# Another order of GpSimd's sums, ScalarE's ReLUs, VectorE's block sums and second-layer products around a seven-product pointwise convolution

## The chip, the core and the metric

The kernel runs on one NeuronCore of a Trainium2 chip. TensorE multiplies matrices into PSUM; VectorE and ScalarE read and write both PSUM and SBUF; GpSimd works on SBUF alone; SyncE issues most of the transfers. Each engine takes its own instructions in the order in which the program has them, and engines wait for each other at semaphores. The metric is the time of one execution on the device in microseconds (us).

## What is computed

Four images of 256 channels and 64x64 points (4096 points each), all in float32. The reference, cut to what matters here:

```python
# layer 0: attention over 4096 points
attn = softmax(q @ k)                       # q, k: 32 channels
x = gamma * (v @ attn.T) + x
# layer 1: clustering, then an MLP and a pointwise convolution
y = x + ls1 * cluster(group_norm(x, gn1_w, gn1_b))
hdn = conv1x1(group_norm(y, gn2_w, gn2_b), mlp_w1, mlp_b1)     # 256 -> 1024
hdn = conv1x1(gelu(hdn), mlp_w2, mlp_b2)                       # 1024 -> 256
y = y + ls2 * hdn
z = relu(batch_norm(y * dw_w))
z = relu(batch_norm(conv1x1(z, pw_w)))                         # 256 -> 256
```

The change lies in the last five lines, the MLP with what follows it.

## The kernel before

The images are worked on one after the other; for each there is an attention stage, a clustering stage and an MLP stage (`mlp`, from line 1144). The order of all instructions is written out by hand: the program runs under a manual schedule, so that each engine's queue is the order in which the Python code issues its instructions.

The MLP stage goes over blocks of 512 points, `nb` = 0 to 7 (image 2 has only blocks 0 to 6 here; its block 7 is done by `late_block` beside the next image's attention). Within a block, `j` = 0 to 3 goes over pairs of 128 hidden channels, `j` and `j + 4`. Each product of two 256-channel operands is done as a 2x2 scheme of seven half-size products in place of eight: the operand's quarters are 128 channels by 256 points (`quarters`), and sums of quarters are formed ahead (`factors`, L1230 to L1233) and block sums behind.

- `first(nb, j, ...)` does the seven first-layer products through `seven` (L1351 is the matmul, `product`). They go into three PSUM buffers called `hp`, `hq` and `hr` with 2, 3 and 2 products, which are taken in turn from a pool of two (`ps_s`). ScalarE copies one product out (L1359), VectorE makes the seven block sums (`plus`, L1342), ScalarE applies gelu to the four quarters of `hs` (L1306), in the order h4, h2, h1, h3.
- The second layer's products lag by one `j`: `second_by_seven` is a generator with seven products (L1266), and GpSimd's four sums of the quarters of `hs` (L1273, L1274, L1279, L1280) between them. `seven` draws from it at four places (`mo`): before `hp`, between `hp` and `hq`, between `hq` and `hr`, and after `hr`. How many products are drawn at each is the tuple `slots`: (0, 2, 2, 3) usually, (3, 1, 2, 1) after a score and at `j` = 2 with a pointwise convolution.
- `finish(nb - 1)` puts the second layer's parts of the block before together, on VectorE during the next block's `j` = 0 and 1: three sums (L1409 to L1411), two scaled sums (L1396, 128x256), and two more (L1396, 128x512), which wait in a list `drips` and are issued one at a time behind a `plus`. The ReLUs of both channel halves (`relu`, L1387, ScalarE) wait in a list `hooks`, which `hook()` empties at the end of `j` = 1.
- `norm(nb + 1)` scales the next block's input on VectorE (L1176, two instructions) and leaves its four sums to GpSimd (`ahead`), issued at `j` = 2's generator. `own` are the four sums for the pointwise convolution of the block before; before the change they are issued one by one in `j` = 1's generator.
- `pointwise(nb - 1)`, at `j` = 2 of the middle blocks, does the pointwise convolution by seven products (buffers `hp_pw`, `hq_pw`, `hr_pw`), with its block sums on VectorE (L1342 too), its ReLUs on ScalarE (L1218) and its outputs sent from SyncE's queue (`leave`).
- In images 0 to 2 the next image's first scores are made in the same stage: after `j` = 3 two PSUM buffers from the same pool of two are filled by `score` (L363), ScalarE copies them to SBUF (L371, L372), and VectorE takes maxima of 512 columns (L376), which wait in a list `maxima` and are issued by `rest()`, one at a call.

Two places say the order of L376 and of the ReLUs:

```python
                if j == 3:
                    rest()
...
                hs = first(nb, j, todo, slots, pw)
                if j != 1:
                    rest()
...
                elif j == 1:
                    assert not drips
                    hook()
```

Of the kernel before, what the change touches and what calls it, by code (L numbers as in the profile page):

```python
# [10 lines left out]
ALU = mybir.AluOpType  # L11
# [5 lines left out]
KC = C // P  # L17
# [28 lines left out]
def attention_then_cluster_block(  # L46
# [17 lines left out]
    nc = tc.nc  # L64
# [1079 lines left out]
    def mlp(b, ys, stats2, fill, nxt, blocks, turned):  # L1144
# [25 lines left out]
        def norm(nb, eng):  # L1170


            pairs[nb] = pr = spool.tile([P, 2, KC, NB], F32, tag="s", name=f"xn2_{b}_{nb}")

            def scaled(k):
                nc.vector.tensor_scalar(  # L1176
                    pr[:, 0, k, :],
                    block(ys, k, nb),
                    ga[:, k : k + 1],
                    gb[:, k : k + 1],  # L1180
                    ALU.mult,
                    ALU.add,
                )

            scaled(0)
            scaled(1)
            return factors(eng, pr[:, 0], pr[:, 1])

        def quarters(t):
            return t[:, 0, :HB], t[:, 0, HB:], t[:, 1, :HB], t[:, 1, HB:]  # L1190
# [34 lines left out]
        def factors(eng, src, dst):  # L1225
# [6 lines left out]
            yield eng.tensor_tensor(t3, e, t2, ALU.subtract)  # L1232
            yield eng.tensor_tensor(t4, t2, g, ALU.subtract)  # L1233

        for _ in norm(0, nc.vector):
            pass
        nc.gpsimd.tensor_tensor(pw_abcd, pw_q[1], pw_q[0], ALU.subtract)
        nc.gpsimd.tensor_tensor(pw_bac, pw_abcd, pw_q[3], ALU.add)
        nc.gpsimd.tensor_tensor(pw_bcd, pw_q[2], pw_abcd, ALU.subtract)
        if nxt:  # L1240
            nxt.q_block(0, nc.sync)

# [15 lines left out]
        def second_by_seven(nb, acc, hs, j, own, ahead):  # L1258


            h1, h2, h3, h4 = quarters(hs)
            one, end = j == 0, j == h_n - 1
            x, y, z, w = acc

            def q(bank, half, a, t, start=False, stop=False):
                return nc.tensor.matmul(  # L1266
                    bank[:, half * HB : (half + 1) * HB], a[:, j], t, start=start, stop=stop
                )

            if j == 1:  # L1270
                next(own, None)
            yield q(x, 1, w3_s, h4, one)
            nc.gpsimd.tensor_tensor(h4, h2, h4, ALU.add)  # L1273
            nc.gpsimd.tensor_tensor(h2, h2, h1, ALU.subtract)  # L1274
            yield q(x, 0, a12_s, h3, stop=end)
            if j == 1:
                next(own, None)
            yield q(y, 0, a11_s, h1, one, end)
            nc.gpsimd.tensor_tensor(h1, h1, h4, ALU.subtract)  # L1279
            nc.gpsimd.tensor_tensor(h3, h1, h3, ALU.add)  # L1280
            if end:
                early(nb, acc)
            if j == 1:
                for _ in own:
                    pass
            if j == 2:
                for _ in ahead:
                    pass
            yield q(z, 0, w7_s, h4, one)
            yield q(z, 1, s1_s, h2, stop=end)  # L1290
            yield q(w, 0, s2_s, h1, one)
            yield q(w, 1, a22_s, h3, stop=end)
# [39 lines left out]
        def seven(n, ws, src, sums, dst, act, todo, slots, meanwhile=lambda: None):  # L1332
            e, f, g, h = quarters(src)
            t2, t4, t3, _ = quarters(sums)
            h1, h2, h3, h4 = dst
            w_p, w_u, w_q, w_u3, w_v, w_p2, w_u4 = ws

            def banks(i):
                return ps_s.tile([P, 2, NB], F32, tag="s", name=f"h{i}_{b}_{n}")

            def plus(dst, ps, term):
                nc.vector.tensor_tensor(dst, ps, term, ALU.add)  # L1342
                if drips:
                    drips.pop(0)()

            def mo(i):
                for _ in range(slots[i]):
                    next(todo, None)

            def product(out, w, x):  # L1350
                nc.tensor.matmul(out, w, x, start=True, stop=True)  # L1351


            mo(0)
            ps = banks("p")
            p, u = ps[:, 0, :HB], ps[:, 1, :HB]
            product(p, w_p, e)
            product(u, w_u, t2)
            nc.scalar.copy(h1, p)  # L1359
            plus(h2, u, h1)  # L1360
            mo(1)
            ps = banks("q")
            q, u, v = ps[:, 0, :HB], ps[:, 1, :HB], ps[:, 0, HB:]
            product(q, w_q, f)
            product(u, w_u3, t3)
            product(v, w_v, h)
            plus(h3, u, h2)
            plus(h4, q, h3)
            act(3, h4)
            plus(h2, q, h2)  # L1370
            plus(h2, v, h2)
            act(1, h2)
            mo(2)
            meanwhile()
            ps = banks("r")
            p, u = ps[:, 0, :HB], ps[:, 1, :HB]
            product(p, w_p2, g)
            product(u, w_u4, t4)
            plus(h1, p, h1)
            act(0, h1)  # L1380
            plus(h3, u, h3)
            act(2, h3)
            mo(3)

        def finish(nb, acc):
            def relu(c):
                nc.scalar.activation(  # L1387
                    pairs[nb][:, 1, c, :],
                    block(ys, c, nb),
                    AF.Relu,  # L1390
                    scale=dw_d[:, c : c + 1],
                    bias=dw_e[:, c : c + 1],
                )

            def scaled(y, term, c):
                nc.vector.scalar_tensor_tensor(y, term, par("ls2", c), y, ALU.mult, ALU.add)  # L1396

            if len(acc) == KC:
                for c in range(KC):
                    scaled(block(ys, c, nb), acc[c], c)  # L1400
                    relu(c)
                return

            _, _, z, w = acc
            p7, p5, p6, p4 = (t[:, i * HB : (i + 1) * HB] for t in (z, w) for i in range(2))
            own = pairs[nb][:, 1]
            d1, d2, d3, d4 = quarters(own)
            y0, y1 = block(ys, 0, nb), block(ys, 1, nb)
            nc.vector.tensor_tensor(d4, p6, d1, ALU.add)  # L1409
            nc.vector.tensor_tensor(d3, p7, d4, ALU.add)  # L1410
            nc.vector.tensor_tensor(d2, p5, d4, ALU.add)  # L1411
            scaled(y1[:, HB:], p5, 1)
            scaled(y1[:, :HB], p4, 1)
            drips.append(lambda: scaled(y0, own[:, 0], 0))
            drips.extend([lambda: None] * 2)
            drips.append(
                lambda: scaled(
                    y1.rearrange("p (x n) -> p x n", x=2),
                    d3.unsqueeze(1).to_broadcast([P, 2, HB]),
                    1,  # L1420
                )
            )
            for c in range(KC):
                hooks.append(lambda c=c: relu(c))

# [2 lines left out]
        def hook():  # L1430
            while hooks:
                hooks.pop(0)()
# [12 lines left out]
        for nb in range(blocks):  # L1445
            end = nb == blocks - 1
            for j in range(4):
                if j == 3:
                    rest()
                pw = (lambda: last(nb - 1, True, nc.gpsimd)) if end and j == 2 else lambda: None  # L1450
                hs = first(nb, j, todo, slots, pw)
                if j != 1:
                    rest()
                if j == 0:
                    if nb:
                        finish(nb - 1, acc)
                    acc = [
                        ps_a.tile([P, NB], F32, tag=f"a{c}", name=f"mo{c}_{b}_{nb}")
                        for c in range(KC)
                    ]  # L1460
                    if not end:
                        acc += [
                            ps_m.tile([P, NB], F32, tag="m", name=f"mo{c}_{b}_{nb}")
                            for c in range(2, 4)
                        ]
                    elif nxt:

                        nc.sync.dma_start(
                            out=a21_s, in_=w2.rearrange("(k p) m -> p k m", p=P)[:, :h_n, P:]
                        )  # L1470
                        nxt.q_block(1, nc.sync)
                elif j == 1:
                    assert not drips
                    hook()
                    if not end:
                        ahead = norm(nb + 1, nc.gpsimd)
                        if nb:
                            own = factors(nc.gpsimd, pairs[nb - 1][:, 1], pairs[nb - 1][:, 0])
                        else:
                            own = iter(())  # L1480
                elif j == 2 and nb and not end:
                    pointwise(nb - 1)
                scored = nxt and (nb, j) in at
# [6 lines left out]
                    slots = (2, 1, 1, 0) if scored else (0, 1, 1, 2)  # L1490
                else:
                    todo = second_by_seven(nb, acc, hs, j, own, ahead)
                    slots = (3, 1, 2, 1) if scored or j == 2 and nb else (0, 2, 2, 3)
        for _ in range(2):
            next(todo)
        if nxt:
# [127 lines left out]
```

## Time and profile before

| | |
|---|---|
| three executions, us | 3406.78, 3405.88, 3409.68; median 3406.78 |
| profiled execution, us | 3409.36 |
| its span, us | 3407.6 |
| mean granted TensorE clock | 0.995 |
| ScalarE busy in the span | 1684.4 us (49%) |
| MLP stages, from the first L1351 to the last, us from the span's start | 656.7 to 895.2, 1501.0 to 1737.6, 2346.5 to 2557.1, 3168.1 to 3392.8 |

How to read it: the page gives for each engine the time in which it was busy, and for each group of instructions its line, engine, operation, the tiles that it writes and reads, the shapes, the count, the busy time, the mean time of one in ns, and the idle time of the engine just before it with what ended it. A float32 matmul stands in the trace as two rows. The timeline has one line for each run of like instructions: start in us, time in us, engine, line, operation, tiles, shapes, count, and in square brackets the wait before it with its releaser. The waits view has one line for each pair of waiter and releaser: total us, times, longest us.

### The profile page before, as it was taken

Reading aid. Unit: us, or ns where it says so; the run is one execution under the profiler, and the core shown is the slowest. Engines: PE = TensorE matmul, PEld = TensorE weight load, DVE = VectorE, ACT = ScalarE, POOL = GpSimd, SP = SyncE. Lnnn points to the kernel's source line nnn. Section 1 sums busy time; section 2 is a strip of 40 time slices with the busy share of each in tenths; the row PEclk is TensorE's granted clock in tenths of the full one; section 3 lists DMA queues with packets and bytes.
Section 4 is the critical chain, followed back from the end, with each engine's and each line's share of the span. In section 5 each row is a group of like instructions: output and inputs, shape, how many; then the busy total and the mean of one; then the engine's idle time right before and its main releaser. Section 6 shows DMA issues by size and latency. Waiting matters only on the chain.

```text
span 3407.6 us, 34726 instructions
## 1 busy us (share of the span) xinstructions
PE 3337.4 (98%) x12322; PEld 1807.4 (53%) x12322; DVE 2220.3 (65%) x3546; ACT 1684.4 (49%) x2253; POOL 1919.1 (56%) x1366
## 2 busy tenths in 40 slices
PE   8999999999999999999999999999999999999999
PEld 4434345777533444577744344466773344445686
DVE  4667664667666766466766676646666766764765
ACT  5555543444555554344455555434545555544444
POOL 2655766356365666546636566654644676573563
PEclk9999999999999999999999999999999999999999
DMA  2000002000000000100000000010000000010000
GB/s 71 13 13 13 13 14 78 4 13 19 25 13 13 13 13 22 70 4 19 16 25 13 10 15 11 22 70 4 19 26 13 13 13 13 11 38 1 13 19 25
DMA packets 43101, 70.98 MB, mean 21 GB/s; under 512 B 9680, under 2 KB 18480, under 8 KB 42928
## 3 DMA queue, kind: packets, MB, share of 16 engines
q1 hardware_dynamic: 38064, 61.94, 5.5%
q10 hardware_dynamic: 4608, 6.30, 0.8%
q8 instruction: 97, 1.59, 0.2%
q0 software_dynamic: 256, 0.52, 0.1%
q14 instruction: 76, 0.62, 0.1%
HBM read 43.46 MB, written 16.89 MB: 18 GB/s over the span
## 4 chain that ended last, share of the span: by engine, by line
PE 85%; DVE 8%; POOL 3%; ACT 2%; issue 1%; DMA 0%; SPq 0%; ACTq 0%; DVEq 0%; POOLq 0%
PE av L477 53%; PE sc L363 8%; PE mo L1266 6%; PE hq L1351 3%; PE vp L314 2%; PE hp L1351 2%; PE fv L861 2%; PE hr L1351 2%; DVE hs L1342 2%; PE mo L1250 1%; DVE x L1396 1%; ACT hs L1306 1%; PE hq_pw L1351 1%; PE pw L1206 1%; DVE top L376 1%
## 5 line engine op out<-in xcount | busy, mean ns | idle before, releaser
L477 PE MATMUL av<-s,v 128*128 128x512 f32 x4096 | 1819.2, 598 | 0.6 <-ACT s L467 0.6
L472 POOL TENSOR_TENSOR acc<-acc,s 128x1024 f32<-128x1024 f32 x448 | 1057.2, 2360 | 538.1 <-ACT s L467 519.3
L477 PEld LDWEIGHTS av<-s,v 128*128 128x128 f32 x4096 | 759.1, 190 | 1044.7 <-issue 1034.7
L467 ACT ACTIVATE s<-s 128x1024 f32<-128x1024 f32 x512 | 540.2, 1057 | 592.6 <-DVE s L464 551.2
L464 DVE TENSOR_TENSOR s<-s,mb 128x1024 f32<-128x1024 f32 x512 | 595.7, 1205 | 19.1 <-ACT mb L448 16.8
L385 DVE TENSOR_TENSOR top<-sc,top 128x1024 f32<-128x1024 f32 x196 | 239.4, 1221 | 374.8 <-PE sc L363 374.6
L1266 PE MATMUL mo<-hs,w 128*128 128x256 f32 x1512 | 401.7, 385 | 6.1 <-POOL hs L1279 3.9
L1306 ACT ACTIVATE hs<-hs,pv_s 128x256 f32<-128x256 f32 x496 | 231.0, 503 | 352.1 <-DVE hs L1342 352.1
L381 ACT COPY s<-sc 128x1024 f32<-128x1024 f32 x224 | 224.8, 1003 | 225.8 <-PE sc L363 225.8
L1266 PEld LDWEIGHTS mo<-hs,w 128*128 128x128 f32 x1512 | 275.3, 190 | 83.0 <-ACT hs L1306 17.7
L363 PE MATMUL sc<-q,k 32*128 32x512 f32 x2048 | 302.5, 640 | 0.5 <-ACT s L386 0.5
L388 DVE TENSOR_TENSOR top<-sc,top 128x1024 f32<-128x1024 f32 x196 | 240.0, 1224 | 72.5 <-ACT s L381 59.4
L386 ACT COPY s<-sc 128x1024 f32<-128x1024 f32 x224 | 227.0, 1013 | 66.2 <-DVE top L383 36.1
L1342 DVE TENSOR_TENSOR hs<-hq,hs 128x256 f32<-128x256 f32 x496 | 198.3, 420 | 69.8 <-PE hq L1351 59.6
L469 POOL TENSOR_TENSOR acc<-s 128x1024 f32<-128x1024 f32 x32 | 75.3, 2354 | 286.4 <-ACT s L467 286.4
L1273 POOL TENSOR_TENSOR hs<-hs 128x256 f32<-128x256 f32 x108 | 78.5, 727 | 209.3 <-PE mo L1266 101.0
L363 PEld LDWEIGHTS sc<-q,k 32*128 32x128 f32 x2048 | 86.4, 182 | 185.7 <-issue 122.0
L1342 DVE TENSOR_TENSOR hs<-hp,hs 128x256 f32<-128x256 f32 x124 | 52.3, 422 | 173.8 <-ACT hs L1359 173.8
L1351 PE MATMUL hr<-xn,w 128*128 128x256 f32 x496 | 128.2, 381 | 1.6 <-DVE hs L1342 1.6
L314 PE MATMUL vp<-wv_s,x 128*128 128x256 f32 x512 | 123.4, 387 | 0.2 <-ACT v L322 0.2
L314 PEld LDWEIGHTS vp<-wv_s,x 128*128 128x128 f32 x512 | 93.5, 190 | 26.2 <-issue 11.2
L1351 PEld LDWEIGHTS hr<-xn,w 128*128 128x128 f32 x496 | 94.9, 192 | 20.7 <-issue 4.8
(261 smaller groups left out, 3513.2 us busy)
## 6 DMA issues: line engine op xcount, KB each, us to landing
x<-in_x SPq DMA_DIRECT2D x32, 512.0 KB, 6.7
out<-xn SPq DMA_DIRECT2D x62, 256.0 KB, 2.1
w<-in_w SPq DMA_DIRECT2D x8, 1024.0 KB, 10.9
mr<-row_mx SPq DMA_DIRECT2D x28, 256.0 KB, 3.1
rden<-row_rd SPq DMA_DIRECT2D x28, 256.0 KB, 3.1
q<-q ACTq DMA_DIRECT2D x96, 64.0 KB, 2.0
mix<-in_wfv SPq DMA_DIRECT2D x8, 192.0 KB, 8.5
q<-q SPq DMA_DIRECT2D x24, 64.0 KB, 2.1
```

The costliest lines, as they stand in the source:

```text
L314: nc.tensor.matmul(vps[0][:, i % 2, :], xs[i * P // XT][:, k, o : o + P], wv_s[:, k, :], start=(k == 0), stop=(k == KC - 1),)
L363: nc.tensor.matmul(halves[r // 2][:, r % 2, :], k_s[rows, g, :], q_s[rows, :], start=True, stop=True)
L385: nc.vector.tensor_tensor(top, halves[1], top, ALU.max)
L388: nc.vector.tensor_tensor(top, halves[0], top, ALU.max)
L464: nc.vector.tensor_tensor(sh, sh, mxs[nb].unsqueeze(1).to_broadcast([P, 2, NB]), ALU.subtract)
L467: nc.scalar.activation(sh, sh, AF.Exp)
L472: nc.gpsimd.tensor_tensor(acc, acc, s[:, 2 * h : 2 * h + 2], ALU.add)
L477: nc.tensor.matmul(av[c], own["v"][:, RG * g + quarter, c * P : (c + 1) * P], slots[u][:, quarter, :], start=(g == 0 and quarter == 0), st ...
L1266: return nc.tensor.matmul(bank[:, half * HB : (half + 1) * HB], a[:, j], t, start=start, stop=stop)
L1306: nc.scalar.activation(src, src, AF.Gelu_apprx_tanh, bias=pvc("b1", P, j + 4 * (i > 1)))
L1342: nc.vector.tensor_tensor(dst, ps, term, ALU.add)
L1351: nc.tensor.matmul(out, w, x, start=True, stop=True)
```

## The change

What it does, by places:

1. `norm` hands its two scalings out as a generator's first part. For block 0, where VectorE does the sums too, the first sum (f - e) stands between the two scalings.
2. The three sums of the pointwise convolution's weights (L1237 to L1239, GpSimd) are no longer issued at the stage's start; they are `own` of block 0, so they are issued in the generator of its `j` = 1.
3. In the generator of `j` = 1, the second of the sums in `own` is no longer issued between L1274 and L1279; the first one stays where it is, and the other three come behind L1280.
4. The ReLU of channel half 0 is issued inside `seven`, after the second gelu (`act(1, h2)`); the ReLU of half 1 stays at the end of `j` = 1 (`rectify`).
5. The second 128x512 sum of `finish` moves one `plus` down in `drips`.
6. `rest()` is called before and after `first` at `j` = 2 and 3, and no more after `j` = 0.
7. The products drawn at `j` = 3 of a middle block are (3, 1, 0, 3) instead of (3, 1, 2, 1).

```diff
-            scaled(0)
-            scaled(1)
-            return factors(eng, pr[:, 0], pr[:, 1])
+            def parts():
+                rest = factors(eng, pr[:, 0], pr[:, 1])
+                scaled(0)
+                if nb == 0:
+                    next(rest)
+                scaled(1)
+                yield
+                yield from rest
+
+            rest = parts()
+            next(rest)
+            return rest
...
+        def left_factors():
+
+            yield nc.gpsimd.tensor_tensor(pw_abcd, pw_q[1], pw_q[0], ALU.subtract)
+            yield nc.gpsimd.tensor_tensor(pw_bac, pw_abcd, pw_q[3], ALU.add)
+            yield nc.gpsimd.tensor_tensor(pw_bcd, pw_q[2], pw_abcd, ALU.subtract)
+
         for _ in norm(0, nc.vector):
             pass
-        nc.gpsimd.tensor_tensor(pw_abcd, pw_q[1], pw_q[0], ALU.subtract)
-        nc.gpsimd.tensor_tensor(pw_bac, pw_abcd, pw_q[3], ALU.add)
-        nc.gpsimd.tensor_tensor(pw_bcd, pw_q[2], pw_abcd, ALU.subtract)
...
             yield q(x, 0, a12_s, h3, stop=end)
-            if j == 1:
-                next(own, None)
             yield q(y, 0, a11_s, h1, one, end)
...
             act(1, h2)
+            hook()
             mo(2)
...
-            drips.extend([lambda: None] * 2)
+            drips.extend([lambda: None] * 3)
...
-            for c in range(KC):
-                hooks.append(lambda c=c: relu(c))
+            hooks.append(lambda: relu(0))
+            return lambda: relu(1)
...
-                if j == 3:
+                if j > 1:
                     rest()
                 pw = (lambda: last(nb - 1, True, nc.gpsimd)) if end and j == 2 else lambda: None
                 hs = first(nb, j, todo, slots, pw)
-                if j != 1:
+                if j > 1:
                     rest()
                 if j == 0:
                     if nb:
-                        finish(nb - 1, acc)
+                        rectify = finish(nb - 1, acc)
...
                 elif j == 1:
-                    assert not drips
-                    hook()
+                    assert not drips and not hooks
+                    if nb:
+                        rectify()
                     if not end:
                         ahead = norm(nb + 1, nc.gpsimd)
                         if nb:
                             own = factors(nc.gpsimd, pairs[nb - 1][:, 1], pairs[nb - 1][:, 0])
                         else:
-                            own = iter(())
+                            own = left_factors()
...
-                    slots = (3, 1, 2, 1) if scored or j == 2 and nb else (0, 2, 2, 3)
+                    slots = (0, 2, 2, 3)
+                    if scored:
+                        slots = (3, 1, 2, 1)
+                    elif j == 2 and nb:
+                        slots = (3, 1, 0, 3)
```

## The prediction

> **What bounds the kernel now.** I read the page first, then the waits, then the timeline of one block (block 3 of image 0), then the same view of blocks 1 and 6 and of image 3. The page:
>
> ```profile
> PE 3337.4 (98%) x12322; PEld 1807.4 (53%) x12322; DVE 2220.3 (65%) x3546; ACT 1684.4 (49%) x2253; POOL 1919.1 (56%) x1366
> ...
> L1266 PE MATMUL mo<-hs,w 128*128 128x256 f32 x1512 | 401.7, 385 | 6.1 <-POOL hs L1279 3.9
> ```
>
> TensorE bounds everything; every other engine has a third of its time free. 98% hides small stops, because a matmul's end is modelled: the second products' row admits 6.1 us of idle time. So I use starts. A 128x256 product is two rows, and undisturbed rows start 0.216 us apart: 0.432 per product. Stops show where a run of n rows is followed later than n x 0.216. The waits view tells who ends them:
>
> ```profile
> PEld hp L1351 <- DVE hs L1342: 17.4, 30, 1.3
> PEld mo L1266 <- POOL hs L1279: 12.3, 21, 0.6
> PEld mo L1266 <- POOL hs L1280: 10.6, 21, 0.5
> ```
>
> 21 times is once per middle block: there are 23 blocks with a seven-product pointwise convolution (1 to 6 of images 0, 1 and 3, 1 to 5 of image 2), less block 6 of images 0 and 1. The timeline of block 3:
>
> ```profile
> 750.06 0.68 DVE L376 TENSOR_TENSOR top<-top,s 128x512 f32<-128x512 f32 x1
> 750.66 0.42 DVE L1409 TENSOR_TENSOR xn<-mo,xn 128x256 f32<-128x256 f32 x1
> ...
> 754.36 1.46 PE L1266 MATMUL mo<-hs,w 128*128 128x256 f32 x6
> 754.67 0.90 DVE L1396 SCALAR_TENSOR_TENSOR x<-xn,pc_s,x 128x512 f32<-128x512 f32 x1
> 755.50 0.41 DVE L1342 TENSOR_TENSOR hs<-hq,hs 128x256 f32<-128x256 f32 x1
> 755.95 1.31 ACT L1306 ACTIVATE hs<-hs,pv_s 128x256 f32<-128x256 f32 x3 [0.98 <-DVE hs L1342]
> 755.97 0.70 PE L1351 MATMUL hp<-xn,w 128*128 128x256 f32 x2
> 756.50 0.59 PE L1351 MATMUL hp<-xn,w_abcd 128*128 128x256 f32 x2
> 757.16 1.50 ACT L1387 ACTIVATE xn<-x,dw_e,dw_d 128x512 f32<-128x512 f32 x2
> 758.03 0.73 POOL L1230 TENSOR_TENSOR xn<-xn 128x256 f32<-128x256 f32 x1 [3.00 <-ACT xn L1387]
> 760.21 0.72 POOL L1231 TENSOR_TENSOR xn<-xn 128x256 f32<-128x256 f32 x1
> 760.90 0.59 PE L1266 MATMUL mo<-hs,w 128*128 128x256 f32 x2
> 760.90 0.72 POOL L1279 TENSOR_TENSOR hs<-hs 128x256 f32<-128x256 f32 x1
> 761.67 1.50 PE L1266 MATMUL mo<-hs,w 128*128 128x256 f32 x4 [0.18 <-POOL hs L1279]
> 761.77 1.20 DVE L376 TENSOR_TENSOR top<-top,s 128x512 f32<-128x512 f32 x1
> 762.38 1.18 POOL L1232 TENSOR_TENSOR xn<-xn 128x256 f32<-128x256 f32 x1
> 763.02 0.59 PE L1351 MATMUL hp_pw<-xn,wpw_s 128*128 128x256 f32 x2
> ```
>
> Six rows from 754.36 should end in a start at 755.66; it is 755.97 (0.31 lost), because hp of j=2 takes the PSUM buffer that VectorE empties with the sum at 755.50, which stood behind the 0.90 of L1396. A restart costs 0.10 more (755.97 to 756.50 is 0.53, not 0.43). Two rows from 760.90 and four from 761.67 cost 0.34 and 0.49: GpSimd's L1279 and L1280 stood behind L1231, a sum of the pointwise convolution's. Small losses (0.045 on gelu, 0.04 on L1273, 0.04 in hr_pw, 0.10 after the score) bring the block to 1.46. In image 3, without scores, it is 1.25.
>
> **What the Trainium skill says.** "SBUF — State Buffer", section "SBUF: two separate sides": VectorE with two SBUF inputs (or in its 2-port mode) and GpSimd take one port pair as an exclusive lock, so the later waits for the whole of the other. The trace agrees: L376 takes 0.68 alone and 1.20 at 761.77 beside L1280; L1232 behind it 1.18, alone 0.72. "ScalarE: Activation LUTs", section "Table sets: the hidden batching unit": relu lies in every table set. The trace agrees: L1387 follows L1306 at 757.16 with no load between, so putting a ReLU between gelus loads nothing. "TensorE: Matmul & The Clock Gate", Specifications: VectorE, ScalarE and GpSimd take instructions strictly in order. The timeline is in program order, and so I count queues.
>
> **The change part by part** (times on block 3's scale, nothing lost earlier).
>
> *L376 leaves the end of j=0, and the second block-sum product (L1396) goes behind the sum at 755.50.* d4 (L1409) starts at 750.06 instead of 750.66. Then rows as they are: five operations to 752.30, L1396 ended at 753.31 since GpSimd's L1274 holds the lock to 752.76, three sums with starts 0.45, 0.34, 0.45 apart, and the one at 755.50 ends at 754.89 instead of 755.91. hp starts at 755.66: 0.41 gone. From there TensorE's products are due 0.432 apart: hp twice, the first two second products at 756.52 and 756.95, hq three from 757.38, two at 758.68 and 759.11, hr two from 759.54, three from 760.40, then hp_pw; from hq on I add the 0.13 of the next step. L1396 then runs 754.81 to 755.55, hr's two sums to 756.23.
>
> *One ReLU goes ahead of the last two gelus.* Starts: gelu 754.93, ReLU 755.33, gelus 756.03 and 756.43 (a ReLU spaces 0.70, a gelu 0.40), ended 756.94; second ReLU ended 757.6. The product on that gelu is due at 756.95. A late producer's end plus about 0.15 is when the run goes on (L1279 ended at 761.62, its product started at 761.67 and lost the restart's 0.10), so 0.13 is lost here, where 0.045 was.
>
> *GpSimd: L1230 can start at 756.2 instead of 758.03, and L1231 goes behind L1279 and L1280.* L1279 waits for a read at TensorE and starts at 759.55, ends 760.28 (due 760.97); L1280 760.35 to 761.08 (due 761.40, allowance 0.15). Both stops, 0.83, go, and L1273's 0.04. What is late next: L1231 to L1233 now run at 761.04 to 763.6, one of them behind the lock of L376. t3 is just in time; the sum of hp_pw, which overwrites t2, waits for L1233's read of it to 763.63, ends 764.05, and hr_pw, due 763.99, starts about 764.21: 0.22 lost where 0.04 was. Behind that sum VectorE has the four hq_pw sums, which wait for hq_pw's end at 764.2 anyway.
>
> *The other L376 goes ahead of hp's sum of j=2,* behind the two L1176. Each may wait for one GpSimd sum: hp's sum ends at about 759.04, hr is due at 759.67. Cover 0.45; past it, one for one.
>
> *Second products of j=2: (3,1,0,3) for (3,1,2,1).* hr of j=3 loses 0.86 of products before it. It needs hp's sum, which follows ScalarE's copy behind the four L1218; I get 768.32 plus 0.15 against 768.96 due: hidden, 0.5 to spare. The score gains: its second half waits for hr's sums, 0.48 now (0.76 of them after hr, one product in between); with three products between, VectorE's four hq sums (1.67) set it: 0.34. Gain 0.13.
>
> *The three weight sums (L1237 to L1239) go from the stage's start into block 0's j=1,* where GpSimd has been idle for 8.4 us at its first sum; they are used a block later. Zero. *Block 0's sums between the two scalings:* the same four operations on one engine, with one more dependent spacing (0.45 against 0.34): +0.1 in images 0 to 2; in image 3, where GpSimd's lock stretches them (2.98 for two L1176), about -0.15. Zero in sum. No DMA moves: the outputs still leave from the same places.
>
> *Sum.* Blocks 1 to 5 of images 0 to 2: 1.46 becomes 0.13 + 0.22 + 0.10, and 0.13 less for the score: 1.14 x 15 = 17.1. Block 6 of images 0 and 1: there L1176 waits for the second ReLU (1.90 for the two at 849.56, and hr stops 1.05); the ReLU comes 0.8 earlier against TensorE, L376 takes 0.7 of it back: hr stops about 0.6; 1.1 x 2 = 2.2. Image 3: no L376, no lock: 1.25 becomes 0.04: 1.2 x 6 = 7.2. Together 26.5: the profiled execution's span 3407.6 becomes 3381.1, its time 3409.4 becomes 3382.9. It was 2.6 over the median, so against the median 3406.8: 3380.3.
>
> Bounds where nothing shows the new order: gelu 0 to 0.5 (L1396 behind a lock), hr_pw 0.04 to 0.75 (two locks), hr of j=2 0 to 0.2, score gain 0 to 0.34. Best 0.14 a block lost, with the score 33 us gained; worst 1.55 a block, the gain left to image 3 and block 6, about 9.
>
> **The rivals.**
> 1. The stops move: at the upper ends, GpSimd's last three sums and the gelus take the place of what went. For it: L376 takes 1.20 in just that place. Against: TensorE's reads, not the lock, set L1279's start. Half the gain: 3394.
> 2. Slower: hr of j=3 loses its cover. ScalarE's copy for hp stands behind L1218, VectorE's sum behind the pw sums; past 0.5 of delay, each us is paid 23 times. Slower by 0.2% needs 2 us late (0.5 cover, 1.15 gain, 0.3): 3414. Against: a lock is 0.5, and four would have to meet.
> 3. No effect: TensorE's stops are made up elsewhere (3406). Against: 0.2 us later every engine waits for TensorE, whose rows are back to back.
>
> **How the numbers follow.** Forecast (3373 to 3388): 68%. Half (3388 to 3400): 20%. No effect: 5%. Slower: 7%. The time is the first's: 3380.3. 0.2% is 6.8 us, about what a measurement of this kernel can tell from no change; so faster 88%, same 5%, slower 7%. The range goes from the best bound, 3373, into the half case to 3396.
>
> **What would show it.** hp of j=2 with no wait; L1279 and L1280 gone from the waits; hr_pw waiting about 0.4 on VectorE's sum; the period between blocks 3 and 4 of image 0 (744.87 to 775.16, 30.29) 29.15, in image 3 27.2 from 28.4. Wrong, if hr of j=3 or j=2 begins to wait, or the gelu's product by 0.3 or more.

## The result, and the profile after

The changed kernel takes 3378.52 us (median of four, 3377.59 to 3378.91); the kernel before, measured beside it, 3408.23 (3405.88 to 3409.97). The ratio is 0.9913, 95% interval 0.9896 to 0.9930: 29.7 us less, where the prediction had 26.5. The profiled execution has a span of 3376.5 us, 31.1 less. The page of the kernel after, at the places that the prediction showed of the one before:

```profile
PE 3318.5 (98%) x12322; PEld 1815.5 (54%) x12322; DVE 2226.3 (66%) x3546; ACT 1687.1 (50%) x2253; POOL 1929.7 (57%) x1366
...
L1278 PE MATMUL mo<-hs,w 128*128 128x256 f32 x1512 | 387.9, 382 | 0.0
```

TensorE is as full as before and bounds the kernel as before; the counts are the same on every engine. The row of the second-layer products (L1266 before, L1278 now) has no idle time before it any more. Of the waits of TensorE's weight loads, those on GpSimd's third and fourth sum of `hs` are gone from the list, that of hp on VectorE's block sums has fallen from 17.4 us in 30 waits to 5.9 in 7, and that of hr_pw has come up from 5.0 us:

```profile
PEld hr_pw L1361 <- DVE xn L1352: 7.3, 23, 0.5
PEld hp L1361 <- DVE hs L1352: 5.9, 7, 1.3
```

The timeline of block 3 of image 0 after the change. L1351 is L1361 here, L1342 is L1352, L1359 is L1369, L1396 is L1407, L1306 is L1316, L1387 is L1398; GpSimd's four sums L1273, L1274, L1279, L1280 are L1285, L1286, L1289, L1290, and L1230 to L1233 are L1239 to L1242. In some of the experiments the lines lie one or two off these:

```profile
747.21 1.01 DVE L1407 SCALAR_TENSOR_TENSOR x<-xn,pc_s,x 128x512 f32<-128x512 f32 x1
748.14 1.66 DVE L1352 TENSOR_TENSOR hs<-hq,hs 128x256 f32<-128x256 f32 x4
749.29 1.46 PE L1278 MATMUL mo<-hs,w 128*128 128x256 f32 x6
...
750.26 0.80 ACT L1398 ACTIVATE xn<-x,dw_e,dw_d 128x512 f32<-128x512 f32 x1
750.58 0.59 PE L1361 MATMUL hp<-xn,w 128*128 128x256 f32 x2
...
751.45 1.17 PE L1278 MATMUL mo<-hs,w 128*128 128x256 f32 x4
...
754.49 0.73 POOL L1289 TENSOR_TENSOR hs<-hs 128x256 f32<-128x256 f32 x1 [0.31 <-PE mo L1278]
...
758.55 0.42 DVE L1352 TENSOR_TENSOR xn<-hp_pw,xn 128x256 f32<-128x256 f32 x1 [1.30 <-POOL xn L1242]
759.03 1.13 PE L1361 MATMUL hr_pw<-xn,wpw_s 128*128 128x256 f32 x4
```

Six rows from 749.29 at 0.216 end at 750.59, and hp of `j` = 2 starts at 750.58: its stop is gone, because VectorE makes the four hq sums in one go (1.66) with no L1407 among them. The four rows from 751.45 take 1.17 where undisturbed ones take 1.03: 0.14 is lost on the last gelu, behind the ReLU at 750.26. Such a loss is written below as the stop itself and the 0.10 of the restart behind it, here 0.04 + 0.10. GpSimd's L1289 waits for TensorE, no longer TensorE for it. What is late next is hr_pw: hp_pw's sum waits 1.30 for GpSimd's L1242, and hr_pw's run of four starts 0.11 late and takes 1.13.

By place, from the starts of TensorE's rows (first to last L1351 or L1361 of a stage, the sum of the four MLP stages 910.4 before, 878.8 after):

| | before | after | difference |
|---|---|---|---|
| period of blocks 1 to 5, images 0 to 2 (15 of them; median) | 30.29 | 29.14 | -1.15, together -17.6 |
| block 6 of images 0 and 1 | 30.81, 30.53 | 29.75, 29.47 | -1.06 each |
| block 6 of image 2 | 31.42 | 30.80 | -0.62 |
| blocks 1 to 6 of image 3 | 28.44 | 27.37 | -1.07, together -6.4 |
| block 0 of images 0 to 3 | 27.20, 25.91, 27.37, 26.70 | 26.05, 26.04, 26.05, 24.30 | -4.7 together |
| outside the MLP stages | 2497.2 | 2497.6 | +0.4 |

### The profile page after: what moved, and what is told of

Read it like the earlier page. It is cut to its first block, busy times and chain, and to the rows that moved or that the text cites. A ratio compares the mean times of both kernels' runs of the same rounds, so it can differ in the third digit from the quotient of the medians.

```text
span 3376.5 us, 34772 instructions
## 1 busy us (share of the span) xinstructions
PE 3318.5 (98%) x12322; PEld 1815.5 (54%) x12322; DVE 2226.3 (66%) x3546; ACT 1687.1 (50%) x2253; POOL 1929.7 (57%) x1366
## 4 chain that ended last, share of the span: by engine, by line
PE 94%; DVE 4%; ACT 1%; POOL 0%; issue 0%; DMA 0%; SPq 0%; ACTq 0%; POOLq 0%; DVEq 0%
PE av L477 53%; PE mo L1278 10%; PE sc L363 8%; PE hq L1361 5%; PE hp L1361 3%; PE hr L1361 3%; PE vp L314 2%; PE fv L861 2%; PE mo L1262 1%; PE hq_pw L1361 1%; PE pw L1215 1%; PE hr_pw L1361 1%; PE op L982 1%; PE hp_pw L1361 1%; PE qp L333 0%; PE kp L291 0%
## 5 line engine op out<-in xcount | busy, mean ns | idle before, releaser
L1316 ACT ACTIVATE hs<-hs,pv_s 128x256 f32<-128x256 f32 x496 | 233.3, 505 | 339.2 <-DVE hs L1352 339.2
L1278 PE MATMUL mo<-hs,w 128*128 128x256 f32 x1512 | 387.9, 382 | 0.0
L1278 PEld LDWEIGHTS mo<-hs,w 128*128 128x128 f32 x1512 | 282.0, 190 | 60.2 <-ACT hs L1316 19.9
L1352 DVE TENSOR_TENSOR hs<-hq,hs 128x256 f32<-128x256 f32 x496 | 198.5, 421 | 75.5 <-PE hq L1361 65.2
L1285 POOL TENSOR_TENSOR hs<-hs 128x256 f32<-128x256 f32 x108 | 82.3, 762 | 194.5 <-ACT hs L1369 91.4
L1352 DVE TENSOR_TENSOR hs<-hp,hs 128x256 f32<-128x256 f32 x124 | 52.1, 420 | 143.0 <-ACT hs L1369 143.0
L1361 PE MATMUL hr<-xn,w 128*128 128x256 f32 x496 | 127.5, 379 | 0.5 <-DVE hs L1352 0.5
L1361 PEld LDWEIGHTS hr<-xn,w 128*128 128x128 f32 x496 | 94.1, 190 | 19.1 <-issue 4.8
```

The costliest lines, as they stand in the source:

```text
L1278: return nc.tensor.matmul(bank[:, half * HB : (half + 1) * HB], a[:, j], t, start=start, stop=stop)
L1316: nc.scalar.activation(src, src, AF.Gelu_apprx_tanh, bias=pvc("b1", P, j + 4 * (i > 1)))
```

## The experiments

Theory: each of parts 3 to 7 moves an instruction past another in one in-order queue, and TensorE's stops go where the forecast put them; what the parts give doesn't add up, since some cover each other. Rivals: one part does nearly everything; or the time comes from elsewhere, such as the stage starts. Nine of the twelve kernels undo one or two parts of the change in the kernel after; three alter the order further. Medians stand against the 3378.5 of the kernel after. The kernel before, run again beside each set of them, had medians from 3407.7 to 3410.6. As the last section shows, the time outside the MLP stages and at the start of a stage differs by some us between kernels whose code there is the same, so I read the mechanism from the periods and use the median for the sum.

| | median, us | sum of the MLP stages, against after | period images 0 to 2 | image 3 | block 6, images 0 and 1 |
|---|---|---|---|---|---|
| after | 3378.5 | 0 | 29.14 | 27.37 | 29.75, 29.47 |
| part 3 undone | 3378.3 | +1.4 | 29.14 | 27.37 | 30.27, 30.00 |
| part 4 undone | 3390.7 | +13.3 | 29.64 | 27.57 | 31.36, 32.75 |
| parts 3 and 4 undone | 3397.2 | +20.0 | 29.72 | 28.11 | 33.04, 32.77 |
| part 6 undone | 3381.6 | +8.0 | 29.48 | 27.37 | 29.69, 29.70 |
| part 5 undone | 3397.7 | +21.1 | 30.06 | 28.28 | 30.74, 30.46 |
| part 7 undone | 3379.4 | +3.3 | 29.28 | 27.37 | 29.89, 29.60 |
| part 2 undone | 3382.8 | +6.9 | 29.14 | 27.37 | 29.75, 29.46 |
| swap | 3373.0 | -2.8 | 28.92 | 27.23 | 30.27, 29.99 |
| parts 5 and 6 undone | 3401.8 | +25.2 | 30.17 | 28.28 | 30.38, 30.38 |
| part 1 undone | 3377.4 | -0.6 | 29.14 | 27.37 | 29.75, 29.46 |
| swap, part 6 undone | 3379.7 | +6.9 | 29.39 | 27.23 | 30.46, 30.17 |
| swap, part 1 undone, L376 of block 6 late | 3369.7 | -5.3 | 28.91 | 27.23 | 29.14, 29.07 |

### Part 3 undone: the second sum of `own` back between L1285/L1286 and L1289

```diff
             yield q(x, 0, a12_s, h3, stop=end)
+            if j == 1:
+                next(own, None)
             yield q(y, 0, a11_s, h1, one, end)
```

> The changed kernel with part 3 undone: the second of the pointwise convolution's sums goes back between GpSimd's second and third sum of hs at j = 2. First theory (each stop has its own cure, and the ReLU put early is what frees GpSimd): with L1239 early, the sum fits the gap before L1289, which waits for TensorE; L1290 is 0.2 to 0.3 late for its product, hr_pw's stop of 0.22 goes; a middle block of images 0 to 2 stays at 29.14 to 29.3 us, the kernel within 3 us of the changed one. Rival (the order on GpSimd is what removed the stops at L1279 and L1280): both stops come back, 0.83 a block in 23 blocks, about 18 us.

3378.34 (3377.96 to 3380.62), ratio to before 0.9909 (0.9894 to 0.9924): no difference, as in the first theory. In block 3 a product waits 0.07 + 0.10 on L1290 again, and the 0.11 + 0.10 in hr_pw fall to 0.04: GpSimd gives back at one end what it takes at the other. Only block 6 is 0.52 longer, at hr.

### Part 4 undone: both ReLUs at the end of `j` = 1

```diff
             act(1, h2)
-            hook()
...
-            hooks.append(lambda: relu(0))
-            return lambda: relu(1)
+            return lambda: (relu(0), relu(1))
```

> The changed kernel with part 4 undone: both ReLUs are issued at the end of j = 1, behind all four gelus. First theory: the stop on the gelu's product (0.14 with its restart) goes, GpSimd's five sums start about 1.1 us later and reach the last product of j = 2 0.1 to 0.2 late, hr_pw's stop grows by 0.2: a middle block of images 0 to 2 becomes 29.2 to 29.6 us instead of 29.14, the kernel 2 to 10 us slower than the changed one. Rival (the early ReLU alone removed the stops at GpSimd's sums): 0.8 a block comes back, about 18 us.

3390.68 (3390.56 to 3391.41), +12.2, more than the first theory allowed and less than the rival. The timeline of its block 3:

```profile
754.64 0.72 POOL L1239 TENSOR_TENSOR xn<-xn 128x256 f32<-128x256 f32 x1 [2.68 <-ACT xn L1397]
...
759.70 0.70 PE L1361 MATMUL hp_pw<-xn,w 128*128 128x256 f32 x2
```

GpSimd's first sum for the pointwise convolution starts at 754.64 and everything behind it is late: the product on L1290 loses 0.16 + 0.10, the second hp_pw (759.70, two rows after 759.06) 0.20 + 0.10. The gelu's 0.14 is saved. So a middle block pays 0.50, in image 3 0.20. The rest is block 6: there the two L1176 wait for the second ReLU, hr stops 2.08 us instead of 0.39, and in image 1 TensorE then runs at half clock for 3.4 us.

### Parts 3 and 4 undone

The two diffs above together.

> The changed kernel with parts 3 and 4 both undone. First theory: if either of them nearly suffices alone, this brings the stops at GpSimd's third and fourth sums back: 0.5 to 0.9 a block in 23 blocks, 11 to 20 us slower than the changed kernel. Rival (VectorE's earlier block sums freed the rest, and GpSimd's queue followed): under 5 us.

3397.24 (3395.56 to 3398.16), +18.7, within the first theory. Its block 3 has the stops of the kernel before back to 0.01: 0.35 + 0.10 and 0.27 + 0.10 at the products on the third and fourth GpSimd sum. That these 0.83 went through GpSimd's order is shown. The parts don't add: 0 for one, 0.50 for the other, 0.58 for both (the gelu's 0.14 and 0.17 in hr_pw go the other way).

### Part 6 undone: L376 back at the end of `j` = 0

```diff
-                if j > 1:
+                if j == 3:
                     rest()
...
-                if j > 1:
+                if j != 1:
                     rest()
```

> The changed kernel with part 6 undone: the maxima L376 go back behind j = 0 and leave the place ahead of hp's sum of j = 2. First theory: d4 starts 0.6 us later, and all of VectorE's j = 1 with it; the sum that frees hp's buffer still ends in time (by 0.03), but the gelu's product stops 0.6 to 0.7 us instead of 0.14: 0.5 to 0.6 more in each of the 17 middle blocks of images 0 to 2, nothing in image 3, which has no maxima: 8 to 10 us. Rival (VectorE's late block sums bounded the whole block, GpSimd included): the whole gain of images 0 to 2 goes, about 19 us.

3381.64 (3376.71 to 3382.33), only +3.1 where the first theory had 8 to 10, and its periods only +0.34 where it had 0.5 to 0.6. hp of `j` = 2 doesn't stop; the stop on the last gelu grows from 0.03 to 0.37. The timeline of its block 3:

```profile
749.28 0.74 DVE L1407 SCALAR_TENSOR_TENSOR x<-xn,pc_s,x 128x512 f32<-128x512 f32 x1
...
753.70 0.70 PE L1278 MATMUL mo<-hs,w 128*128 128x256 f32 x2 [0.20 <-ACT hs L1316]
```

L376 puts 0.60 in front of VectorE, but L1407 then starts behind GpSimd's L1286 and takes 0.74 where it takes 1.01 beside it in the kernel after: 0.27 comes back, 0.33 is left, and TensorE pays that at the gelu. Of the +8.0 in the MLP stages 5.1 are these (15 x 0.34), and 2.3 are at image 3's start; 4.0 came back outside the stages, where TensorE ran at half clock for 20.7 us in this profile and for 28.9 in that of the kernel after.

### Part 5 undone: the second 128x512 block-sum product one place earlier

```diff
-            drips.extend([lambda: None] * 3)
+            drips.extend([lambda: None] * 2)
```

> The changed kernel with part 5 undone: the second 128x512 sum of the block before goes back ahead of the sum that frees hp's buffer at j = 2. First theory: that sum ends about 0.75 us later, hp stops by 0.1 to 0.3 with its restart, and the gelus behind the early ReLU come late, so that their product stops by 0.4 to 0.6: 0.5 to 0.8 a block in all 23 middle blocks, image 3 too: 12 to 18 us slower than the changed kernel. Rival (with the maxima gone from j = 0 there is slack for it): under 3 us.

3397.74 (3395.26 to 3401.35), ratio 0.9965 (0.9953 to 0.9976), +19.2: the dearest single part, a little above what the first theory allowed. The timeline of its block 3:

```profile
752.15 1.12 DVE L1407 SCALAR_TENSOR_TENSOR x<-xn,pc_s,x 128x512 f32<-128x512 f32 x1
753.19 0.41 DVE L1352 TENSOR_TENSOR hs<-hq,hs 128x256 f32<-128x256 f32 x1
753.66 0.70 PE L1361 MATMUL hp<-xn,w 128*128 128x256 f32 x2
...
755.70 0.70 PE L1278 MATMUL mo<-hs,w 128*128 128x256 f32 x2 [0.48 <-ACT hs L1316]
```

L1407 runs before the last hq sum, behind GpSimd's lock (1.12). hp, which needs that sum, stops 0.19 + 0.10; then the gelus, with a ReLU between them, are late by 0.65 + 0.10 where 0.03 + 0.10 were. Part 4, which is good for GpSimd, makes part 5 necessary: in the kernel before, without a ReLU ahead of the gelus, the same position cost only the stop at hp (the gelu's was 0.04), while with parts 5 and 6 both undone, below, the gelu's 0.65 is there too.

### Part 7 undone: (3, 1, 2, 1) at `j` = 3

```diff
-                        slots = (3, 1, 0, 3)
+                        slots = (3, 1, 2, 1)
```

> The changed kernel with part 7 undone: products of j = 2 drawn as (3, 1, 2, 1) again. First theory: the score waits for hr's block sums again, 0.14 more in each of the 17 middle blocks of images 0 to 2, nothing in image 3: 2.4 us. Rival (the products behind hr also covered a wait of hp or hq of the next block, or hr's missing cover cost something that now comes back): image 3 changes too, or the difference is over 4 us or below zero.

3379.37 (3377.07 to 3382.21), +0.9. The whole difference of a middle block is in `j` = 3, 7.78 for 7.64: 0.14 x 17 = 2.4, as in the first theory, and image 3 keeps its period. The median alone wouldn't show it.

### Part 2 undone: the three weight sums back at the stage's start

```diff
         for _ in norm(0, nc.vector):
             pass
+        for _ in left_factors():
+            pass
...
-                            own = left_factors()
+                            own = iter(())
```

> The changed kernel with part 2 undone: the three sums of the pointwise convolution's weights go back to the stage's start on GpSimd. First theory (from the two traces, not from the forecast, which had zero): GpSimd's sums hold the port pair while VectorE makes the scale of the group norm, so L263 and L264 take 0.5 us each again instead of 0.23 and hp starts about 0.68 us later in images 0 to 2, 0.5 to 1.5 in image 3: 2.5 to 3.5 us; all middle blocks as in the changed kernel. Rival: the earlier start came from part 1 (the sum between the two scalings), and nothing changes here.

3382.82 (3378.56 to 3386.13), +4.3, a little above the first theory. No period of a middle block moves; the stage starts do. The same VectorE instruction at image 0's start, first with the weight sums (this kernel), then without (the kernel after):

```profile
654.97 0.54 DVE L263 TENSOR_SCALAR ga_gn<-pc_s,rstd_gn 128x2 f32<-128x2 f32 x1
```

```profile
654.15 0.23 DVE L263 TENSOR_SCALAR ga_gn<-pc_s,rstd_gn 128x2 f32<-128x2 f32 x1
```

An instruction on two columns more than doubles in length beside GpSimd's (L264 behind it too, 0.49 for 0.22), and L1176 and the first hp stand behind them: in the kernel after the first hp comes 2.17 after the group norm's matmul (653.10 to 655.27), here 2.84 (653.92 to 656.76). In image 2 it is the same; in image 1 the sums come later, L263 takes 0.23 and L264 0.29, and the first hp 2.46. On top of that, in this kernel's profile a stretch at half clock falls into the first products of all of images 0, 1 and 2, as in two of them before and in none after. The windows view of its image 0 (columns: window, length, busy time and count of PE, PEld, DVE, ACT, POOL, granted clock):

```profile
655.50:658.90 3.40, 1.37 (x5) 0.95 (x6) 3.21 (x8) 1.88 (x3) 0.87 (x2) 0.99 0.00 0
658.90:662.30 3.40, 3.40 (x9) 2.69 (x9) 1.28 (x4) 0.37 (x1) 0.00 (x0) 0.50 0.00 0
```

After 3.4 us with TensorE busy for 1.37, the next 3.4 us are granted half the clock. These stretches follow the weight sums. In every trace of this case half clock begins on a grid of 3.413 us (last section). Cut along that grid, the emptiest window at the starts of images 0, 1 and 2 has TensorE busy for 1.33, 1.40 and 1.15 us here, and half clock follows each time; in the kernel before it is 1.28, 1.93 and 1.28, and half clock follows in images 0 and 2. In the other twelve kernels, without the weight sums there, it is 1.8 to 2.1 in all 36 starts, and half clock follows none. So undoing part 2 makes block 0 of images 0, 1 and 2 longer by 1.2, 1.6 and 1.7 too.

### The swap: the product on h1 ahead of that on h3

```diff
-            yield q(x, 0, a12_s, h3, stop=end)
             yield q(y, 0, a11_s, h1, one, end)
+            yield q(x, 0, a12_s, h3, stop=end)
```

> The changed kernel with one thing more: in the generator of the second layer the product on h1 is drawn before the product on h3. First theory: the gelu of h3 gets over 1 us of cover, so its stop of 0.14 goes in 23 middle blocks; GpSimd's third sum, which waits for the read of h1, starts 0.4 to 1.5 us earlier, so that the pointwise convolution's sums are done before hp_pw's block sum needs them, and hr_pw's stop falls from 0.22 to 0.04: 0.3 a block in images 0 to 2 and 0.13 in image 3, 5 to 7 us faster than the changed kernel. Rival (hr_pw waits for VectorE's copy and sum, not for GpSimd): only the gelu's stop goes, 3 us.

3372.98 (3372.79 to 3373.07), ratio 0.9892 (0.9877 to 0.9908), -5.5. h1 is one gelu earlier than h3, so the last gelu has 0.43 more time: its stop of 0.03 + 0.10 is gone, hr_pw has 0.08 less, 29.14 becomes 28.92. That is less than the first theory's 0.3, and its 5 to 7 us were met in part by chance: the periods give 15 x 0.22 + 6 x 0.14 = 4.1, block 6 takes 1.0 of it back, and the rest lies outside the MLP stages. Block 6 is 0.52 longer. Its timeline in image 0:

```profile
840.96 0.79 POOL L1289 TENSOR_TENSOR hs<-hs 128x256 f32<-128x256 f32 x1
841.09 1.21 DVE L376 TENSOR_TENSOR top<-top,s 128x512 f32<-128x512 f32 x1
842.22 0.41 DVE L1352 TENSOR_TENSOR hs<-hp,hs 128x256 f32<-128x256 f32 x1
842.68 1.13 PE L1361 MATMUL hr<-xn,w 128*128 128x256 f32 x4 [0.89 <-DVE hs L1352]
```

L1289 comes earlier too, starts just ahead of L376 and locks it (1.21 for 0.68), and hr waits for the sum behind.

### Parts 5 and 6 undone

> The kernel after with parts 5 and 6 both undone: the 128x512 block-sum product one place earlier, and L376 back at the end of j = 0. All theories against the kernel after (3378.5 us); part 5 undone alone gave 3397.7, part 6 alone 3381.6. First theory (VectorE's queue at j = 1 decides, and L376's 0.60 is partly paid by the lock that L1407 then misses): hp of j = 2 stops for 0.31 + 0.10 as in the kernel before, the product on the last gelu still stops for about 0.75, so a middle block costs 1.0 more in images 0 to 2 and 0.9 more in image 3: 15 x 1.0 + 6 x 0.9 = 20.4, so 3399. Rival (the two costs add, since each delays VectorE by its own length): 15 x 1.26 + 6 x 0.9 = 24.3, so 3403. Second rival (they overlap wholly, the later one hides the other): 3397.7, with periods of 30.06 as in part 5 undone alone.

3401.81 (3400.02 to 3403.27), +23.3. Periods of 30.17 and 28.28 (+1.03 and +0.91), hp stops 0.31 + 0.10 and the gelu 0.65 + 0.10, each as in the first theory; with 15 x 1.03 + 6 x 0.91 = 20.9 its sum held too (the rival's 1.26 a block did not), and the rest is in blocks 6 and 7 (0.6 to 0.9 each), which it had not counted. The 0.41 at hp takes L376 and L1407 together: L376 alone at its old place makes no stop at hp, L1407 alone 0.19 + 0.10.

### Part 1 undone: both scalings of block 0 ahead of its sums

```diff
                 scaled(0)
-                if nb == 0:
-                    next(rest)
                 scaled(1)
```

> The kernel after with part 1 undone: both scalings of block 0 ahead of its four sums. First theory: the same operations on one engine, so only the dependent spacing moves: 0.13 less at the starts of images 0 to 2, and about 1.0 more in image 3, where the scalings stand behind GpSimd's lock: +0.6 in sum, so 3379.1 against 3378.5, periods of the middle blocks unchanged. Rival (image 3's start is covered by something that comes later anyway, so nothing comes back there): -0.4, so 3378.1. Second rival (the longer under-use at the start of image 3 brings a stretch at half clock into the products): +3 or more, so 3381.

3377.44 (3377.33 to 3378.23), -1.1. The starts of images 0 to 2 are 0.13 shorter each, and image 3's is not longer: its second hp product stops 1.64 where it stops 1.81 in the kernel after. The first theory had 1.0 more at image 3; the rival, that nothing comes back there, held. Part 1 gains nothing.

### The swap with part 6 undone

The diffs of both.

> The kernel after with the second-layer product on h1 drawn ahead of that on h3, and L376 back at the end of j = 0. With the swap alone 3373.0 us. First theory: L376 no longer stands ahead of hp's sum, so block 6 of images 0 and 1 loses its stop at hr (1.05 + 0.10 each, 2.3 in sum); in the middle blocks VectorE is 0.33 later with the gelus, of which the swap covers all but some 0.07 + 0.10 at the product on h1: 15 x 0.17 = 2.6 given back. Together +0.3: 3373.3. Rival (the 0.33 comes through whole, as with the products in their old order): 15 x 0.33 - 2.3 = +2.7: 3375.7. Second rival (the swap covers it all): -2.3: 3370.7.

3379.69 (3379.65 to 3381.46), +6.7 over the swap alone, where the three theories had +0.3, +2.7 and -2.3: none of them. The timeline of its block 3:

```profile
749.26 0.73 POOL L1289 TENSOR_TENSOR hs<-hs 128x256 f32<-128x256 f32 x1
749.32 1.22 DVE L1407 SCALAR_TENSOR_TENSOR x<-xn,pc_s,x 128x512 f32<-128x512 f32 x1
```

The swap puts L1289 0.5 earlier, just ahead of the L1407 that L376 has delayed: 1.22 instead of 0.74, so the 0.27 that had paid for part of L376 turns into a loss of 0.21. hp and the gelu's product stop for 0.09 + 0.10 and 0.25 + 0.10.

### The swap, part 1 undone, and L376 of block 6 after hr

The swap and part 1's diff, and:

```diff
-                if j > 1:
+                late = nb == NBLK - 2 and j == 2
+                if j > 1 and not late:
                     rest()
...
                 if j > 1:
                     rest()
+                if late:
+                    rest()
```

> The kernel after with the products on h1 and h3 swapped (alone: 3373.0 us), the scalings of block 0 ahead of the sums again (alone: 1.1 below the kernel after), and, in block 6 alone, L376 moved from before hp of j = 2 to after hr. First theory (the hr stop of block 6, 1.05 + 0.10, is L376 on VectorE ahead of hp's sum, locked by GpSimd's L1289): with L376 away hp's sum ends 1.2 earlier and the stop is gone in images 0 and 1, 2.3 in sum; the scalings give 0.4 to 0.6: 3370.2, periods of block 6 of 29.1 and 28.8 where the swap alone has 30.27 and 29.99. Rival (the second ReLU ahead of the two L1176 sets it, L376 only stands behind): block 6 as with the swap alone, 3372.5. Second rival (two L376 in a row after hr come between hp_pw's product and its sum, and hr_pw stops for 0.7): about half of the gain, 3371.5.

3369.65 (3368.23 to 3373.11), ratio to before 0.9890 (0.9873 to 0.9906): faster than both kernels (its slowest execution is 4.5 below the fastest of the kernel after), and the first theory of block 6 holds, with 29.14 and 29.07 where it had 29.1 and 28.8. Its timeline there (L1350 and L1359 are L1352 and L1361 of the kernel after):

```profile
839.90 0.41 DVE L1350 TENSOR_TENSOR hs<-hp,hs 128x256 f32<-128x256 f32 x1
840.44 1.05 PE L1359 MATMUL hr<-xn,w 128*128 128x256 f32 x4
```

From the start of the block the sum ends 1.1 us earlier than with the swap alone (the block itself starts 1.2 earlier too), and hr starts 0.03 late in place of 1.05.

## Why the prediction was right

The direction, the place and the size of the gain in the middle blocks came out: it forecast a period of 29.15 and the trace has 29.14. By its steps:

- **hp of `j` = 2, 0.41**: gone as forecast. The prediction took L376 and L1396 together; undone singly and jointly they show that moving L1396 was enough for hp (with L376 back alone there is no stop), and that moving L376 alone would have left 0.19 + 0.10. Even the lock it counted on (L1396 ended late by L1274) is there: 1.01.
- **One ReLU ahead of the last gelus, 0.13**: 0.14 measured. It forecast this for images 0 to 2 and left it out of image 3, where 0.03 + 0.10 are paid too; so image 3 gave 6.4, not 7.2, and its period came to 27.37, not 27.2.
- **GpSimd, 0.83, and hr_pw 0.22 late next**: both as forecast (0.21 in hr_pw), shown by undoing parts 3 and 4.
- **L376 ahead of hp's sum**: no wait in the middle blocks. In block 6, hr stops 0.39 + 0.10 for the 0.6 forecast, and the two blocks gave 1.06 each for 1.1.
- **Second products (3, 1, 0, 3)**: 0.13 forecast, 0.14 measured, and hr of `j` = 3 kept its cover, so the slower rival had nothing to work on.
- **The weight sums, "Zero"**: the term that was mis-sized. The prediction asked who waits for GpSimd where the sums go, and not who was locked where they come from. That is 0.7 ahead of the first product in each of images 0 to 2, and the profile before had it: L263 took 0.54 there and L264 0.49. It is also the half clock in the first products of images 0 and 2, whose block 0 took 27.20 and 27.37 where image 1, with none, took 25.91. Undoing part 2 alone brings the delay back (0.67 at images 0 and 2, 0.29 at image 1) and the half clock in all three, and costs 4.3 in the median. The Trainium skill, "SBUF — State Buffer", section "SBUF: two separate sides", states the exclusive lock that the prediction had itself applied to L376; an instruction of two columns pays it too (L263 takes 0.54 for 0.23 beside a 128x128 sum of 0.46).
- **Block 0's sums between the scalings, "Zero in sum"**: +0.13 in three images, as forecast, but nothing came back in image 3.
- **Not forecast**: image 2's block 6 (-0.62; undoing part 6 brings 0.39 of it back, parts 5 and 6 all), and block 0 of image 3 (-2.4, with half clock in it before and none after).

What was counted came to 26.1 us for the 26.5 forecast (17.6 + 2.1 + 6.4); image 2's block 6 and the four blocks 0, which were not, brought 0.6 and 4.7. In images 0 and 2 the shorter block 0 comes with the weight sums, as undoing part 2 shows. In image 3 it stays open: 2.4 came off block 0, but the first product came 1.7 later after image 2's last (612.6 for 611.0), and block 0 of image 3 came out at 24.0 to 26.6 in kernels with the same code there. Outside the stages the profile after is 0.4 longer, though 0.7 was saved ahead of three first products: TensorE was at half clock there for 28.9 us, in the profile before for 23.8, and no edit accounts for that. So the terms of the forecast made 26.1 of the 31.1 us between the two profiles; the rest it did not see.

## What to carry to other kernels

Before an instruction is moved in an in-order queue, ask both what it will stand in front of and what it frees where it stood, and for VectorE and GpSimd ask the same of the port lock, since an instruction's length depends on what runs beside it. Parts of a reordering don't add up: one was worth nothing and another 19 us, depending on the cover that the others had left, so undo them in pairs as well as singly. Where the rows of the bound engine are at an even pitch, the gaps between their starts give differences of 0.1 us a block, which the median of the whole kernel hides.

## What the runs showed of the hardware

TensorE's clock was granted at half in stretches of 3.41 or 6.83 us, with rows 0.427 apart for 0.216. Within each of the fourteen traces the stretches start on one grid of 3.413 us, to 0.005 us over the whole kernel. The Trainium skill, "TensorE: Matmul & The Clock Gate", section "Part 1: The HAM clock gate (the "warmup" mystery)", has a free-running window of about 3.4 us, after which an idle array is clocked at half; the length and the grid agree. But it takes less than an idle window. With parts 3 and 4 undone, one gap of 2.29 us between two starts in block 6 of image 0 (845.41 to 847.70) lies in one window but for 0.2, and the next window is at half clock:

```profile
845.60:849.01 3.41, 1.50 (x7) 1.18 (x7) 3.24 (x7) 0.34 (x1) 3.33 (x5) 1.00 0.00 0
849.01:852.42 3.41, 3.41 (x10) 2.70 (x9) 1.68 (x4) 1.48 (x4) 1.06 (x2) 0.50 0.00 0
```

With part 4 alone undone a gap of the same length (845.34 to 847.63) is cut in two by the grid, and no half clock follows:

```profile
843.24:846.65 3.41, 2.48 (x12) 1.73 (x10) 2.43 (x3) 1.20 (x3) 2.94 (x4) 1.00 0.00 0
846.65:850.07 3.42, 2.44 (x11) 2.18 (x12) 3.25 (x9) 1.19 (x3) 3.20 (x5) 1.00 0.00 0
```

The first of these blocks took 33.04, the second 31.36 with the same stop at hr: such a stretch costs some 1.6 us, and whether it is paid depends on where the gap falls. In image 1 both kernels have the gap in one window (1.50 and 1.51 us busy), and both are followed by half clock. The busy time of the window is not the whole rule: at image 3's start with part 7 undone, 1.44 us was not followed by half clock.

The time between the MLP stages of images 0 and 1 (from the last first-layer product to the next first one) is touched by part 2 alone. In the twelve kernels that keep part 2 it came out within 0.1 of 605.2, 606.7 or 608.2, with no stretch, 3.41 us or 6.83 us at half clock in it: steps of 1.5 us that no edit explains, and the reason why a difference of 3 us between two medians says little here. With the weight sums at the stage's start it was 605.85 (the kernel before, no stretch) and 608.4 (part 2 undone, 6.83 us), 0.7 and 0.2 above a step.
